# A graph network on one Trainium2 core: the second q projection and the second layer's neighbour sums as seven block products, a chunk transposed elsewhere, other banks for the root products

## The chip, the cores and the metric

The kernel runs on one core of one Trainium2 chip. A core has five engines with instruction streams of their own: TensorE (PE) multiplies matrices, VectorE (DVE) and ScalarE (ACT) do elementwise work and read PE's results out of its accumulation memory (PSUM, eight banks of 512 fp32 columns per partition), GpSimdE (POOL) does elementwise work in SBUF and issues indirect transfers, and SyncE (SP) issues transfers. PE's weight loads are listed apart as PEld. The metric is device time in microseconds: the median of three runs is 746.15 us (744.75 to 747.71). All data are fp32.

## The reference

With N = 384 nodes of 1024 features, the program computes `x = x + attention(relu(layernorm(x)))` and then `x = x + rgcn(relu(layernorm(x)))`.

The attention has two projections in a row for each of q, k and v, all 1024 by 1024:

```python
q = x @ wq.T + bq
q2 = (q @ wiq.T + biq)          # likewise k, k2 and v, v2
scores = einsum(q2, k2) * scale + mask    # 16 heads of 64; mask from 12672 typed edges
out = softmax(scores) @ v2, then @ wo.T + bo
```

The graph network projects to 768 features (`w_in`), runs two layers, and projects back (`w_out`) with a layer norm. A layer is, for six relations whose weights are combinations of four bases,

```python
W = einsum('rb,bio->rio', comp, basis)
x = relu(sum over edges of (x[src] @ W[type]) / count + x @ root + bias) + h_in
x = batchnorm(x)                # over the 384 nodes, per feature
```

## The kernel before, in words

Activations are kept transposed, features on the partitions: a 1024-feature tensor is 8 chunks of 128 features by 384 nodes, a 768-feature one 6 chunks. PE, POOL, SP and DVE run in exactly the order in which the program issues instructions; ACT is ordered by the scheduler in the first part of the program and by hand in the rest.

**Block products.** Many products are done as two by two blocks with seven instead of eight block multiplications (the Strassen-Winograd form): the inputs are halved over the contraction and over the 192 + 192 nodes, and two output chunks stand beside each other. The sums of weights (S, four, `output_sums`, line 367) and of activations (T1 to T4, `node_sum`, line 360) are made by DVE ahead of the products. Four of the seven products share accumulations in the banks pa, pb, pc, and the results are read out between them: ACT copies with the bias (lines 491, 492, 495, 512) and DVE additions (497, 503, 505). The last product of a part, with T4, is kept as `rest` and issued two products into the next part (line 493), after DVE's addition of line 503 has freed its bank. k, k2 and v are done so (loop at line 475; `multiply`, line 374, issues four matmuls of 192 columns). q and q2 are done by `project` (line 384), in whole products: per part of 256 output features, 2 x 8 matmuls of 384 columns (line 395).

**The adjacency.** The generator `edge_steps` (line 173) interleaves the building of two tables with the projections: each `fill(1)` runs one step. `find_cells` (line 232, DVE, two times 4 to 12 comparisons of 128 by 128 per call) finds the edges that hit the same cell; its results feed 198 indirect transfers on POOL (`put_mask`, line 261, and `put_count`, line 266). SP clears the tables (line 271) and loads the keys (line 238) in the same steps. The mask is read back for the softmax (lines 305 to 315); the counts become A, loaded by lines 657 to 661, divided per relation by `share` (line 335: PE sums, DVE reciprocal, POOL multiplication at line 342) and combined into At for the four bases by `mix` (line 319, on DVE, the first relation on ACT).

**Transition.** After attention, the output projection (line 616, the last half row in two pieces at line 688) adds to x row chunk by row chunk; each row chunk of 128 nodes is normalised into xn and transposed by PE with `relu_T` (line 157) into h2T, copied by ACT and DVE. The w_in products (`first_products`, line 718, and the loop from 731) need h2T.

**The layers** (loop at line 827). For each basis, H = x times basis, again in seven block products in five banks (lines 832 to 867), kept as 3 node chunks by 768 features. Then the root product into six banks pr, one for each output chunk (line 880; banks are taken from a ring, leaving out the bank `kept` of the pending `rest`), and on top, in the same banks, the neighbour sums: for each output chunk 12 matmuls of 384 columns over 4 bases and 3 node chunks (line 895, `add_neighbours`), first bases 0 and 1 for all chunks, then 2 and 3. As each chunk ends, ACT adds the bias and takes the Relu into `u` (line 905), DVE adds the input and normalises (lines 906 to 918). `go_between` puts the shares and mixes between the products. After the second layer come the output products (line 939), the layer norm and the store (line 954).

Weights pass through five buffers in the order of `wload`, issued by SP, which waits where a buffer is not free.

Of the kernel before, what the change touches and what calls it, by code (L numbers as in the profile page):

```python
# [51 lines left out]
def gnn_kernel(ctx: ExitStack, tc: tile.TileContext, out, x, edges, chunks, cols, rows, small,  # L52
# [294 lines left out]
    with ExitStack() as inner:  # L347
# [36 lines left out]
        def project(w, src, bias, name, on_part=None, on_start=None):  # L384

            dst = act_tile(name)
            for part in range(4):
# [12 lines left out]
                for o in range(2):  # L400
                    oc = part * 2 + o
                    nc.scalar.activation(dst[:, oc, :], ps[o][:, :N], AF.Identity,
                                         bias=cols_sb[:, bias + oc:bias + oc + 1])
                if on_part:
                    on_part(part)
                fill(1)
# [9 lines left out]
        with tc.tile_pool(name="edge", bufs=1, side="right") as ep:  # L416
# [32 lines left out]
            q = project(wq, hT, BQ, "q", on_start=last_chunk)  # L449
# [5 lines left out]
            plan = [(*i, part) for i in (("k", wk, BK), ("k2", wik, BIK), ("v", wv, BV)) for part in range(4)]  # L455
# [9 lines left out]
            def at_the_end(part):  # L465
                if part == 3:
                    for i in (1, 2, 3, 4):
                        node_sum(T, i, hT, sum_tile(i))
                    prepare()

            q2 = project(wiq, q, BIQ, "q2", at_the_end)
# [3 lines left out]
            for n, (name, w, bias, part) in enumerate(plan):  # L475
                src = made["k"] if name == "k2" else hT
# [4 lines left out]
                if n == 2:  # L481
                    nc.sync.dma_start(boB, rows[R_BO:R_BO + 1, :].to_broadcast([P, D]))
                if n < 10:
                    fill(1)
# [34 lines left out]
            k2, v = made["k2"], made["v"]  # L519
# [158 lines left out]
        for t in range(NT):  # L678
            last = t == NT - 1
            for half in range(2):  # L680
# [29 lines left out]
                add_y(half * 512, ps)  # L710
            norm(t, xn[:, t, :], *row_spread(st), parts=2 if last else 1)
            if not last:
                output_sums(a[t], S[t])
            if t:
                relu_T(h2T, t - 1, xn[:, t - 1, :])
# [49 lines left out]
    with tc.tile_pool(name="conv", bufs=1) as cp:  # L765
# [61 lines left out]
        for l in range(L):  # L827

            H_ = []
            rest = lambda: None  # L830
            for b in range(B):
                H_.append(cp.tile([P, NT, DC], F32, tag="H", name="H", bufs=4))
                hs = [[H_[b][:, n, i * HC:(i + 1) * HC] for i in range(2)] for n in range(NT)]
                pe, pf, pb, pc, pa = [next_bank("ps_g")[:, :N] for _ in range(5)]
                kept = ring[-1]
# [41 lines left out]
            pr = [next_bank("ps_c", [i for i in range(8) if i != kept])[:, :N] for _ in range(KC)]  # L877
            for k in range(KC):
                for o in range(KC):
                    nc.tensor.matmul(pr[o], w[k // 2][:, k % 2, o * P:(o + 1) * P], XT[:, k, :], start=(k == 0), stop=False)  # L880
                if k == 0:
                    rest()
                go_between(l, B, k)
            if l + 1 < L:
                w = load_basis(l + 1, 0)
            else:

                rowsB = late.tile([P, 3, D], F32, tag="A", name="rowsB")
# [3 lines left out]
            def add_neighbours(o, bs):  # L892
                for b in bs:
                    for n in range(NT):
                        nc.tensor.matmul(pr[o], H_[b][:, n, o * P:(o + 1) * P], At[:, b, n, :],  # L895
                                         start=False, stop=(b == B - 1 and n == NT - 1))

            for o in range(KC):
                add_neighbours(o, (0, 1))
            for o in range(KC):  # L900
                add_neighbours(o, (2, 3))
                ps = pr[o]
                c = l * KC + o
                u = cp.tile([P, N], F32, tag="u", name="u", bufs=2)
                nc.scalar.activation(u, ps, AF.Relu, bias=cols_sb[:, CB + c:CB + c + 1])  # L905
                nc.vector.tensor_tensor(XN[:, o, :], u, XT[:, o, :], ALU.add)  # L906
# [6 lines left out]
                nc.scalar.activation(sc[:, 0:1], sc[:, 0:1], AF.Sqrt)  # L913
                nc.vector.reciprocal(sc[:, 0:1], sc[:, 0:1])
# [4 lines left out]
                if o == 2 and l + 1 < L:  # L919
                    T = weight_sums(w)  # L920
# [7 lines left out]
        w = [wload(w_out[part], "w_out") for part in range(3)]  # L928
        for t in range(NT):
            hf = cp.tile([P, NT * DC], F32, tag="H", name="hf", bufs=4)[:, :D]  # L930
# [86 lines left out]
```

## Time and profile before

| | |
|---|---|
| median of three runs | 746.15 us |
| profiled execution, its own time | 747.49 us |
| its span | 745.7 us |
| mean granted PE clock | 0.994 |
| q projection on PE | about 13 to 56.9 us |
| q2 | 56.9 to 98.2 us |
| k, k2, v | 98.2 to 211 us |
| second v, attention | 211 to 312 us |
| output projection, transposes, w_in products | 312 to 388 us |
| layer 0: basis products, root, neighbours | 388 to 480, 477 to 506, 506 to 552 us |
| layer 1: the same | 552 to 641, 636 to 661, 661 to 707 us |
| output products, norm, store | 707 to 746 us |

How to read the profile: the first part of its page has the busy time of each engine; a digit in its second part is the busy share of a fortieth of the span in tenths. A row of the groups gives line, engine, operation, output and inputs, shapes and count, then the busy time, the mean of one in ns, and the engine's idle time ahead of them. A row in order of time gives start, duration (both us), engine, line, operation and count, and in brackets how long the engine was idle before it and what ended that. A row of windows gives, for a stretch, each engine's busy time with the count of instructions, then the granted PE clock, the DMA share and GB/s. A matmul of fp32 leaves two records. Ends of matmuls are modelled, so starts are the surer measure of pace.

### The profile page before, as it was taken

What the parts mean: (1) busy time and instruction counts of PE and PEld (TensorE: products, weight loads), DVE (VectorE), ACT (ScalarE), POOL (GpSimd) and SP (SyncE); (2) the same over time, 40 slices, a digit from 0 to 9 for tenths busy, and PEclk for the clock granted to TensorE, in tenths of its full rate; (3) what the DMA queues carried; (4) which work ended last, traced back from release to release, by engine and by line L of the source; (5) the groups of instructions that cost most, each with busy time, mean ns of one, the idle gap of its engine ahead of it and who ended that gap; (6) DMA issues with size and microseconds to landing.
All of it is one profiled execution on the core that took longest, in us unless ns stands there. A gap on an engine that the chain in (4) does not pass through costs nothing.

```text
span 745.7 us, 7797 instructions
## 1 busy us (share of the span) xinstructions
PE 724.6 (97%) x2820; PEld 471.6 (63%) x2820; DVE 435.3 (58%) x1161; ACT 141.8 (19%) x324; POOL 321.0 (43%) x242
## 2 busy tenths in 40 slices
PE   8999999999999999999899999899999999999995
PEld 7755589999964444446885555555555555555543
DVE  5878518878405499444524699980287766000655
ACT  3301021111102377410121130100022111000200
POOL 1355767778786787587774464210000000210000
PEclk9999999999999999999999999999999999999999
DMA  7797677644356322624428943321003312700001
GB/s 294 254 346 247 190 183 210 202 148 112 114 145 208 57 2 2 212 1 85 86 1 208 277 149 128 127 84 43 0 1 127 113 67 82 289 1 0 0 29 56
DMA packets 40532, 90.94 MB, mean 122 GB/s; under 512 B 19644, under 2 KB 27680, under 8 KB 36270
## 3 DMA queue, kind: packets, MB, share of 16 engines
q1 hardware_dynamic: 18478, 79.62, 30.4%
q0 software_dynamic: 21008, 8.42, 10.3%
q10 hardware_dynamic: 1008, 2.41, 0.8%
q8 instruction: 22, 0.36, 0.2%
q14 instruction: 16, 0.13, 0.0%
HBM read 79.27 MB, written 11.16 MB: 121 GB/s over the span
## 4 chain that ended last, share of the span: by engine, by line
PE 87%; DVE 10%; issue 1%; ACT 1%; DMA 0%; DVEq 0%; ACTq 0%
PE ps_c L895 12%; PE ps_g L846 12%; PE ps_q L395 11%; PE ps_g L840 9%; PE ps_k L377 7%; PE ps_c L880 6%; PE ps_v L525 6%; PE ps_y L616 5%; PE ps_f L939 4%; PE ps_v L377 4%; PE ps_s L564 3%; PE ps_x L377 3%; PE ps_o L609 2%; PE ps_pT L598 2%; DVE same L250 2%; DVE At L326 2%
## 5 line engine op out<-in xcount | busy, mean ns | idle before, releaser
L266 POOL DMA_INDIRECT atab<-count,at x99 | 159.2, 1608 | 55.8 <-DMA atab<-count,at 30.0
L261 POOL DMA_INDIRECT mtab<-m_val,at x99 | 102.3, 1034 | 58.5 <-issue 23.5
L895 PE MATMUL ps_c<-At,H 128*128 128x384 f32 x288 | 93.2, 486 | 0.0
L895 PEld LDWEIGHTS ps_c<-At,H 128*128 128x128 f32 x288 | 54.7, 190 | 38.2
L927 POOL TENSOR_TENSOR x_sb<-x_sb,rowsB 128x1024 f32<-128x1024 f32 x3 | 6.9, 2342 | 159.9 <-DMA rowsB<-in_rows 159.9
L326 DVE SCALAR_TENSOR_TENSOR At<-A,small_sb,At 128x1152 f32<-128x1152 f32 x40 | 62.9, 1635 | 0.0
L840 PE MATMUL ps_g<-T,S 128*128 128x384 f32 x144 | 49.1, 486 | 0.0
L846 PE MATMUL ps_g<-w_c,XT 128*128 128x384 f32 x144 | 48.0, 487 | 0.9 <-DVE H L861 0.9
L846 PE MATMUL ps_g<-w_c,XN 128*128 128x384 f32 x144 | 47.6, 486 | 0.0
L395 PE MATMUL ps_q<-hT,w_q 128*128 128x384 f32 (+1 forms) x160 | 43.4, 436 | 1.4 <-ACT hT L90 1.4
L525 PE MATMUL ps_v<-w_v,v 128*128 128x512 f32 x96 | 41.9, 594 | 0.0
L395 PE MATMUL ps_q<-q,w_q 128*128 128x384 f32 x128 | 41.4, 486 | 0.0
L846 PEld LDWEIGHTS ps_g<-w_c,XT 128*128 128x128 f32 x144 | 27.2, 190 | 20.1 <-DVE H L861 1.5
L846 PEld LDWEIGHTS ps_g<-w_c,XN 128*128 128x128 f32 x144 | 27.4, 190 | 19.1
L840 PEld LDWEIGHTS ps_g<-T,S 128*128 128x128 f32 x144 | 27.4, 190 | 19.1
L395 PEld LDWEIGHTS ps_q<-hT,w_q 128*128 128x128 f32 x160 | 30.2, 200 | 14.1 <-ACT hT L90 1.7
L906 DVE TENSOR_TENSOR XN<-u,XN 128x384 f32<-128x384 f32 x6 | 3.4, 558 | 56.3 <-ACT u L905 56.3
L395 PEld LDWEIGHTS ps_q<-q,w_q 128*128 128x128 f32 x128 | 24.3, 190 | 17.0
L616 PE MATMUL ps_y<-w_o,attT 128*128 128x512 f32 x80 | 35.0, 595 | 0.0
L377 PE MATMUL ps_k<-T,S 128*128 128x192 f32 x192 | 35.0, 326 | 0.0
L342 POOL TENSOR_TENSOR A<-A,rn 128x1152 f32<-128x1152 f32 x6 | 20.1, 3354 | 30.7 <-DVE rn L341 30.7
L577 DVE CUSTOM_DVE_ANT_0 s<-ps_s,mask 128x384 f32<-128x384 f32 x48 | 24.5, 548 | 14.3 <-PE ps_s L564 14.3
(212 smaller groups left out, 1184.2 us busy)
## 6 DMA issues: line engine op xcount, KB each, us to landing
w_c<-in_basis SPq DMA_DIRECT2D x24, 768.0 KB, 6.1
atab<-zero SPq DMA_DIRECT2D x12, 576.0 KB, 7.6
A<-atab POOLq DMA_DIRECT2D x10, 576.0 KB, 10.2
w_c<-in_root SPq DMA_DIRECT2D x6, 768.0 KB, 6.0
w_q<-in_wq SPq DMA_DIRECT2D x4, 1024.0 KB, 11.6
w_q<-in_wiq SPq DMA_DIRECT2D x4, 1024.0 KB, 12.6
w_k<-in_wk SPq DMA_DIRECT2D x4, 1024.0 KB, 5.7
w_k<-in_wik SPq DMA_DIRECT2D x4, 1024.0 KB, 6.2
```

The lines of the kernel that those rows point to most:

```text
L261: nc.gpsimd.indirect_dma_start(mtab[c // PER][:, :], bass.IndirectOffsetOnAxis(at[:, 0, c:c + 1], 0), m_val[:, c:c + 1], None)
L266: nc.gpsimd.indirect_dma_start(atab[0 if i < 18 - DEALT else i % 2][:, :], bass.IndirectOffsetOnAxis(at[:, 1, c:c + 1], 0), count[:, 1, c: ...
L326: nc.vector.scalar_tensor_tensor(At[:, b], A[:, r], w, At[:, b], ALU.mult, ALU.add)
L377: nc.tensor.matmul(ps, a[:, k, :], b[:, k, :], start=start and k == 0, stop=(k == 3), skip_group_check=not start)
L395: nc.tensor.matmul(ps[o][:, c], wt_[:, k, o * P:(o + 1) * P], src[:, k, c], start=(k == 0 and c.start == 0), stop=(k == KD - 1 and c.stop ...
L525: nc.tensor.matmul(ps, v[:, k, t * P:(t + 1) * P], w[k // 4][:, k % 4, :], start=(k == 0), stop=(k == KD - 1))
L616: nc.tensor.matmul(ps, attT[:, k, t * P:(t + 1) * P], w_o[half][k // 4][:, k % 4, :], start=(k == 0), stop=(k == KD - 1))
L840: nc.tensor.matmul(ps, x[:, c], y(c), start=start and c == 0, stop=(c == 2), skip_group_check=not start)
L846: nc.tensor.matmul(ps, block(XT, n, i)[:, c], w[c][:, i, o * HC:(o + 1) * HC], start=(first and c == 0), stop=(c == 2 and (i == 1 or ps is ...
L880: nc.tensor.matmul(pr[o], w[k // 2][:, k % 2, o * P:(o + 1) * P], XT[:, k, :], start=(k == 0), stop=False)
L895: nc.tensor.matmul(pr[o], H_[b][:, n, o * P:(o + 1) * P], At[:, b, n, :], start=False, stop=(b == B - 1 and n == NT - 1))
L939: nc.tensor.matmul(p, XT[:, k, t * P:(t + 1) * P], w[k // 2][:, k % 2, c0:c1], start=(k == 0), stop=(k == KC - 1))
```

## The change

1. `project` is used for q only. q2 becomes the first of the names in the block-product loop: 16 parts instead of 12, with weights prepared one part ahead. The T sums over q are made in `project`'s callback (T1 after part 2, the others and the first S after part 3, behind that part's `fill`), those over hT at the end of q2 as at the end of k2. The `fill` steps keep their place in the count: four in q, then one a part.
2. `relu_T` of the middle chunk of h2T is issued after the first half of the last row's output product, and so ahead of that row's last two pieces and its normalisation.
3. The four H tiles become one. The root products leave out two banks of the pending basis product instead of one.
4. In both layers ACT writes the biased sum into XN instead of `u`. In the second layer, the neighbour sums become seven block products for each pair of output chunks: contraction halved into bases 0, 1 and 2, 3; nodes into 192 + 192. Sums of At (T1 to T4) and of H (four a pair, made one pair ahead) are made by DVE; `take` adds a block product from its bank into XN; the Relu is a step of its own on ACT, and the batch norm of a chunk is split into `measure` and `normalise_layer`, placed between the takes. The freed tiles A, hT and mask8 hold the sums.

```diff
-                if on_part:
-                    on_part(part)
-                fill(1)
+                fill(1)
+                if on_part:
+                    on_part(part, dst)
...
-            q = project(wq, hT, BQ, "q", on_start=last_chunk)
...
-            plan = [(*i, part) for i in (("k", wk, BK), ("k2", wik, BIK), ("v", wv, BV)) for part in range(4)]
+            plan = [(*i, part) for i in (("q2", wiq, BIQ), ("k", wk, BK), ("k2", wik, BIK), ("v", wv, BV)) for part in range(4)]
...
-            def at_the_end(part):
+            def sums_of_q(part, q):
                 if part == 3:
-                    for i in (1, 2, 3, 4):
-                        node_sum(T, i, hT, sum_tile(i))
                     prepare()
-
-            q2 = project(wiq, q, BIQ, "q2", at_the_end)
+                for i in {2: (1,), 3: (2, 3, 4)}.get(part, ()):
+                    node_sum(T, i, q, sum_tile(i))
+
+            q = project(wq, hT, BQ, "q", sums_of_q, on_start=last_chunk)
...
-                src = made["k"] if name == "k2" else hT
+                src = {"q2": q, "k2": made.get("k")}.get(name, hT)
...
-                if n == 2:
+                if n == 6:
                     nc.sync.dma_start(boB, rows[R_BO:R_BO + 1, :].to_broadcast([P, D]))
-                if n < 10:
+                if n < 14:
                     fill(1)
...
                 add_y(half * 512, ps)
+                if last:
+                    relu_T(h2T, t - 1, xn[:, t - 1, :], (0, 1))
...
-            if t:
-                relu_T(h2T, t - 1, xn[:, t - 1, :])
+            if t == 1:
+                relu_T(h2T, 0, xn[:, 0, :], (0, 1))
...
-                kept = ring[-1]
+                kept = ring[-2:]
...
-            pr = [next_bank("ps_c", [i for i in range(8) if i != kept])[:, :N] for _ in range(KC)]
+            pr = [next_bank("ps_c", [i for i in range(8) if i not in kept])[:, :N] for _ in range(KC)]
...
+            def begin(o, func=AF.Identity):
+                c = l * KC + o
+                nc.scalar.activation(XN[:, o, :], pr[o], func, bias=cols_sb[:, CB + c:CB + c + 1])
+
+            if l + 1 < L:
+                for o in range(KC):
+                    add_neighbours(o, (0, 1))
+                for o in range(KC):
+                    add_neighbours(o, (2, 3))
+                    begin(o, AF.Relu)
+                    normalise_layer(*measure(o))
+                    if o == 2:
+                        T = weight_sums(w)
+            else:
...
+                nc.vector.tensor_tensor(T1, q(0, 1), q(0, 0), ALU.subtract)
+                nc.vector.tensor_tensor(T2, q(1, 1), T1, ALU.subtract)
+                T3 = q(0, 1)
+                nc.vector.tensor_tensor(T3, q(1, 1), q(0, 1), ALU.subtract)
+                nc.vector.tensor_tensor(T4, q(1, 0), T2, ALU.subtract)
...
+                pa = first_of(0)
+                for p in range(pairs):
+                    times(pr[2 * p][:, :HN], h(2 * p, 1), q(1, 0))
+                for o in range(KC):
+                    begin(o)
+                take(0, 0, pa)
+                ready = None
+                for p in range(pairs):
+                    last = p == pairs - 1
+                    sums = iter(()) if last else feature_sums(p + 1)
+                    o0, o1 = 2 * p, 2 * p + 1
+                    pc = next_bank("ps_c")[:, :HN]
+                    times(pc, S[p][0], T1, True)
+                    take(o1, 1, pc)
+                    if ready:
+                        normalise_layer(*ready)
+                    next(sums, None)
+                    times(pa, S[p][1], T2)
+                    take(o0, 1, pa)
+                    next(sums, None)
+                    times(pc, S[p][3], q(1, 1))
+                    take(o0, 1, pc)
+                    ready = measure(rectify(o0))
+                    if last:
...
+                    times(pa, S[p][2], T3)
+                    take(o1, 1, pa)
+                    normalise_layer(*ready)
+                    for _ in sums:
+                        pass
+                    following = first_of(p + 1)
+                    times(pa, h(o1, 1), T4)
+                    take(o1, 0, pa)
+                    take(o1 + 1, 0, following)
+                    ready = measure(rectify(o1))
+                    pa = following
```

## The prediction

> **What bounds the kernel now.** I read the busy shares first, then the costliest groups, then the order of time on TensorE (PE), then the queues that feed it. The first two lines are engine shares and PE by fortieths of the span.
>
> ```profile
> PE 724.6 (97%) x2820; PEld 471.6 (63%) x2820; DVE 435.3 (58%) x1161; ACT 141.8 (19%) x324; POOL 321.0 (43%) x242
> PE   8999999999999999999899999899999999999995
> ```
>
> PE is never idle for long: its waits by name come to 12 us of the 745.7 us span. So a part of the change is worth what it takes out of PE's stream, less the waits that it puts there. The two groups that the change rewrites:
>
> ```profile
> L895 PE MATMUL ps_c<-At,H 128*128 128x384 f32 x288 | 93.2, 486 | 0.0
> L395 PE MATMUL ps_q<-q,w_q 128*128 128x384 f32 x128 | 41.4, 486 | 0.0
> ```
>
> A source matmul leaves two records. 144 records of the second layer's L895 run from 660.80 for 46.44 us: 322.5 ns a record, 645 ns a matmul of 384 columns. The same arithmetic with 192 columns runs in the k projection; PE in order of time there (start, us, what):
>
> ```profile
> 98.22 1.46 PE L377 MATMUL ps_k<-hT,w_k 128*128 128x192 f32 x8
> 99.52 2.76 PE L377 MATMUL ps_k<-T,S 128*128 128x192 f32 x16
> ```
>
> Starts are 1.30 us apart per eight records: 162.5 ns a record, 325 ns a matmul. Seven half-width products for eight therefore cost 7/8 x 325/322.5 = 0.882.
>
> **A rule against it.** The Trainium skill, page "TensorE: Matmul & The Clock Gate", section "Back-to-back issue gap", says that in a stream of weight loads and matmuls both set the spacing, so narrow matmuls fall behind their own streaming time. A load here lasts 190 ns, more than 162.5. If it set the pace, 112 + 126 matmuls (476 records) would cost 27.5 ns more each, 13.1 us, and the gain below would be gone. But in the windows, from 98.4 to 116.0, loads and matmuls are both busy all the time at the 162.5 ns pace:
>
> ```profile
> 98.40:116.00 17.60, 17.60 (x110) 17.60 (x110) 4.88 (x11) 3.53 (x8) 12.28 (x11) 1.00 0.65 167
> ```
>
> The loads overlap one another; I use 162.5.
>
> **Part 1, q2 in block products.** Before: 64 matmuls x 645 ns = 41.3 us. After: 4 parts x 7 products x 4 = 112 x 325 ns = 36.4 us: **-4.9 us**. Added on VectorE (DVE), per part: four weight sums (0.68 us each, 0.61 apart: 2.5 us) and three additions (0.35); once, four sums over q (0.95 each); the four over hT move from the start to the end of q2. That is some 18 us more DVE work between 43 and 106 us. Where it lies:
> - Entry. DVE ends find_cells(3) at 51.7 now; with T1 of q (0.95) ahead of it, about 52.7. S of part 0 is done at 55.2 (its weights were issued at 37.2 and land in about 12.6). T2 needs q's last chunk, copied 57.14 to 57.72, so it is ready at 58.7, T3 at 59.6, T4 at 60.5. PE, free at 56.9, has two products of 1.30 before it needs T2, at 59.5. Nothing waits; with find_cells(3) late by more than 3 us, PE would.
> - find_cells(4) and find_cells(5) run at 56.9 and 79.6 now, in DVE time that is otherwise empty. In the new order they stand among q2's additions, which free PE's banks. The one in part 2 lies as find_cells(6) does in k today, where PE waited 0.31: **+0.3**.
> - The hand-over q2 to k is new. Its model is the hand-over k to k2, first DVE, then PE:
>
> ```profile
> 135.43 0.95 DVE L364 TENSOR_TENSOR T<-k 128x768 f32<-128x768 f32 x1
> ...
> 138.84 0.75 DVE L241 TENSOR_SCALAR cells<-keys 128x1152 int32<-128x1152 int32 x1
> ...
> 146.54 0.35 DVE L503 TENSOR_TENSOR k<-k,ps_k 128x192 f32<-128x192 f32 x1
> ```
>
> ```profile
> 146.95 1.57 PE L377 MATMUL ps_k<-T,w_k 128*128 128x192 f32 x8 [1.19 <-DVE k L503]
> ```
>
> Behind the T sums, S and a find_cells of 9 rows (138.84 to 145.41, 6.57 us), the L503 addition is late and PE's T4 product waits 1.19. At q2 to k the step holds find_cells(5), 12 rows; one of that size took 118.19 to 126.63, 8.44. 1.19 + 1.87 = **+3.1 us**. Behind it on PE stand only that part's other products, whose readers on ACT and DVE have time. Ends: 0 if DVE arrives 3 us earlier, 4 if its sums run late.
>
> Part 1: -4.9 + 0.3 + 3.1 = **-1.5**. The moved steps issue the same loads, clears and key loads on SP; each weight load only stands one fill earlier, and keys 4 move behind the last q2 load (46.8), to land near 60 for a use at 77. POOL's scatters wait for find_cells results: find_cells(4) will be done at 85 for a first scatter at 91.7, find_cells(5) at 105 for 116.
>
> **What an earlier PE meets.** POOL issues 198 scatters without pause and cannot follow PE:
>
> ```profile
> 388.99 1.55 POOL L266 DMA_INDIRECT atab<-count,at  x1 [0.30 <-issue]
> 396.99 1.36 POOL L659 DMA_DIRECT2D A<-atab  x1 [6.45 <-PE ps_g L846]
> ...
> 430.31 1.00 POOL L333 TENSOR_TENSOR sum<-sum,A 128x384 f32<-128x384 f32 x1
> ```
>
> The tightest meeting is share(2): its sum is ready at 431.3, PE uses it at 436.08. Slack 4.8 us, against the 1.5 + 2.8 = 4.3 that parts 1 and 2 bring by then: nothing is absorbed, narrowly. Earlier, mask8 is finished at 235.1 and first used at 239.37: slack 4.3 against part 1's 1.5.
>
> **Part 2, the middle chunk.** Now its transposes (354.91) and their copies, behind the last normalisation on DVE, precede the first product:
>
> ```profile
> 354.91 1.04 PE L162 MATMUL ps_h<-ident,xn 128*128 128x128 f32 x8
> 358.65 2.84 PE L377 MATMUL ps_x<-h2T,w_x 128*128 128x192 f32 x16 [2.71 <-issue]
> ```
>
> After: the transposes (0.87) stand at 348.0, their copies end near 350.4 under 6.9 us of L688 products. Those end at 355.8, the first products run to 358.4, and DVE's chain to the first half of xn (355.11 to 357.45 now, 0.87 later) ends at 358.3. The last transposes then end at 359.3; now 362.2. **-2.8 us** (2.4 if the second half is waited for in full).
>
> **Part 3, root banks.** In layer 0 the fourth root product waits 2.20 us for L853, which stands behind two At mixes on DVE. Followed through the ring of banks, the new set still puts that bank fourth and swaps only the fifth and sixth (free by 482.25, used at 482.2). **0**, +-0.1. Here the skill's clock rule bears too (same page, Part 1: half clock after about 3.4 us of idleness). The trace differs; in these windows the third number from the end is PE's granted clock:
>
> ```profile
> 478.00:481.00 3.00, 0.80 (x4) 0.19 (x2) 3.00 (x3) 0.00 (x0) 1.18 (x1) 0.96 0.71 291
> 481.00:482.00 1.00, 1.00 (x2) 0.70 (x3) 1.00 (x3) 0.00 (x0) 0.00 (x0) 0.50 0.00 0
> ```
>
> An idle time of 2.20 was followed by half clock to 484.2, some 1.8 us lost; 2.71 at 356 was not. By the rule the new 3.1 us wait costs nothing more, by this row 1.8. I take 0, by the row nearest in length, and keep 1.8.
>
> **Part 4, neighbours of layer 1.** 72 x 645 = 46.4 us become 3 pairs x 7 x 6 = 126 x 325 = 41.0: **-5.5**. The four sums of At (1152 elements, 1.3 each from the slope between 0.68 at 512 and 0.95 at 768) and the first pair's four (0.95) are 9 us, under the root products from 641 to 660.8, where DVE is empty. Inside, DVE has per pair six additions (0.35), four sums (0.95) and two of these chains (the batch norm of one chunk):
>
> ```profile
> 688.54 0.56 DVE L906 TENSOR_TENSOR XN<-u,XN 128x384 f32<-128x384 f32 x1 [52.30 <-ACT u L905]
> ...
> 691.15 0.48 DVE L918 TENSOR_SCALAR XN<-XN,sc 128x384 f32<-128x384 f32 x1
> ```
>
> 3.1 us each, plus about 0.6 waiting for the new Relu on ACT: 2.1 + 3.8 + 6.2 + 1.2, less overlap of issue, near 12.5 us against PE's 7 x 1.95 = 13.65. Laid out step by step, each addition is in time by 0.1 to 1 us; with every DVE duration 10% longer PE loses 1.4, with 20% longer 3.2. The output product starts with chunks 0 to 3 (6.9 us), and chunk 5 is normalised 4.8 after PE's last product (3.8 now): covered.
>
> **Sum.** -1.5 - 2.8 + 0 - 5.5 = -9.8 us. The profiled execution (747.49, span 745.7) would be 737.7 with span 735.9; on the median 746.15 I predict **736.4 us**.
>
> **Rivals.**
> - DVE paces the neighbours (against: the layout above fits; for: slack of 0.1): gives back 2 to 4, 739.4. Chance 0.16.
> - The scatters end later, through the added two-input DVE sums or shifted transfers, and the 4.3 of parts 1 and 2 are absorbed before layer 0: 740.7. For: slack 0.5; against: DVE is itself late there (PE waits 0.93 and 2.20 on it), which hides a late share. 0.12.
> - No hand-over wait, perhaps no half clock: 731.5 to 733.3. 0.08.
> - Weight loads pace the narrow products, in q2 and neighbours alike: -9.8 + 13.1, **749.5, slower**. It eats the whole gain from 183 ns a record; the k row speaks against. 0.03.
> - The middle chunk's gain reappears as a wait for xn: 739.2; DVE's chain would have to be 2.6 us longer. 0.03.
> - The forecast: 0.58.
>
> From about 0.5% (3.7 us) a measurement can tell a change. Only the loads case is slower, mostly by more than that; where two of the small losses meet, the time ends within, 0.04. Low: 733.0 (no hand-over wait). High: 741.0 (scatters absorb). Faster 0.94, same 0.04, slower 0.02.
>
> **What would show it.** PE's stream of 112 and 126 half-width matmuls at 162.5 ns a record; a wait on L503's successor of about 3 us at the second k part; no 2.7 us gap before the first w_in product; waits in the neighbours summing under 1 us; the 2.20 wait unchanged. Wrong if share(2) or L853 gains a wait as long as the early gain, if the neighbours' waits on the additions exceed 2 us, or if q2's entry waits.

## The result and the profile after

The changed kernel takes **736.71 us** (median of four runs, 735.77 to 738.39) against 746.04 (744.75 to 747.71) for the kernel before on the same chip: a ratio of 0.9874, 95% interval 0.9848 to 0.9900. The forecast was 736.4. The profiled execution has a span of 734.0 us; before it was 745.7. All medians and ratios here and below leave out the runs of a kernel that took over 1.5% longer than its fastest run.

The engine shares and PE by fortieths of the span, from the page of the changed kernel: PE is as full as before (97%), so the time left PE's stream. 11.1 us less of busy PE, 37.6 us more of busy DVE.

```profile
PE 713.5 (97%) x3024; PEld 496.8 (68%) x3024; DVE 472.9 (64%) x1228; ACT 147.2 (20%) x338; POOL 323.3 (44%) x242
...
PE   8999989999999999999999999899999999999995
```

**The neighbours of layer 1.** PE in order of time: the root products end, and 252 half-width records follow without an idle time until the output products at 695.36 (start, us, what; an idle time would stand in brackets). The last two rows are those of before: where the neighbours begin and where the output products follow.

```profile
654.40 7.96 PE L947 MATMUL ps_c<-At,H 128*128 128x192 f32 x48
...
671.96 2.11 PE L947 MATMUL ps_c<-T,H 128*128 128x192 f32 x12
673.90 4.06 PE L947 MATMUL ps_c<-room,room 128*128 128x192 f32 x24
...
695.36 4.88 PE L1054 MATMUL ps_f<-w_out,XN 128*128 128x512 f32 x11
```

```profile
660.64 19.84 PE L895 MATMUL ps_c<-At,H 128*128 128x384 f32 x61
...
707.08 13.47 PE L939 MATMUL ps_f<-w_out,XN 128*128 128x512 f32 x31
```

695.36 - 654.40 = 41.0 us, 162.5 ns a record; before, 707.08 - 660.64 = 46.4.

**The middle chunk.** PE again. The transposes stand ahead of the L687 products, and between these and the w_in products there is no gap; before, 2.71 us.

```profile
347.01 1.04 PE L162 MATMUL ps_h<-ident,xn 128*128 128x128 f32 x8
347.88 7.07 PE L687 MATMUL ps_y<-w_o,attT 128*128 128x256 f32 x32
354.79 2.76 PE L377 MATMUL ps_x<-h2T,w_x 128*128 128x192 f32 x16
357.43 1.11 PE L162 MATMUL ps_h<-ident,xn 128*128 128x128 f32 x8
```

**The hand-over from q2 to k.** DVE in order of time, then PE, then the windows of PE's clock (the third number from the end).

```profile
95.89 0.95 DVE L241 TENSOR_SCALAR cells<-keys 128x1536 int32<-128x1536 int32 x1
...
104.24 0.17 DVE L255 TENSOR_TENSOR at<-off,own 128x12 int32<-128x12 f32 x1
104.33 0.95 DVE L364 TENSOR_TENSOR T<-hT,T 128x768 f32<-128x768 f32 x1
105.19 0.35 DVE L496 TENSOR_TENSOR k<-k,ps_k 128x192 f32<-128x192 f32 x1
105.46 0.34 DVE L502 TENSOR_TENSOR k<-k,ps_k 128x192 f32<-128x192 f32 x1
```

```profile
105.86 2.61 PE L377 MATMUL ps_k<-T,w_k 128*128 128x192 f32 x8 [2.92 <-DVE k L502]
```

```profile
106.00:108.00 2.00, 2.00 (x8) 2.00 (x9) 1.97 (x5) 0.00 (x0) 1.70 (x2) 0.56 0.13 1
108.00:110.00 2.00, 2.00 (x9) 2.00 (x8) 0.60 (x1) 0.42 (x1) 1.39 (x3) 0.59 0.20 17
110.00:112.00 2.00, 2.00 (x14) 2.00 (x13) 0.19 (x1) 0.42 (x1) 1.70 (x2) 1.00 0.81 266
```

The wait is the one forecast (3.1), for the reason forecast: find_cells(5) holds DVE from 95.89 to 104.4, and the additions that free PE's bank stand behind it. What was not booked is the half clock after it. The trace's record of the granted clock gives it 3.41 us, so it costs half of that, 1.7.

**The root bank** still waits, but no half clock follows this time:

```profile
476.18 2.31 PE L880 MATMUL ps_c<-XT,w_c 128*128 128x384 f32 x6 [2.19 <-DVE H L853]
```

A balance by stages, from the starts of PE's first product in each, in us (q2's last product is issued inside the k stage):

| stage | before | after | difference |
|---|---|---|---|
| start to q2 | 56.9 | 55.4 | -1.5 |
| q2, k, k2, v | 153.8 | 154.4 | +0.6 |
| second v, attention, output | 147.9 | 145.0 | -2.9 |
| w_in products | 29.7 | 29.7 | 0 |
| layer 0 to its neighbours | 117.5 | 115.1 | -2.4 |
| neighbours 0, layer 1 to its neighbours | 154.8 | 154.8 | 0 |
| neighbours 1 | 46.4 | 41.0 | -5.5 |
| output products to the end | 38.6 | 38.6 | 0 |

The sum is -11.7. Two rows are not the change's doing. In the first, the execution before happened to run its first 16 q records at half clock (4.52 us for 2.84, at 13 us); in the fifth, it had the half clock after the root wait, and a wait of 0.9 on L861 which the other lacks. The other rows come to -7.8. Half clocks of 3.41 us come and go from one execution to the next (the last section shows what decides), so the worth of the parts has to be found one by one.

### The profile page after: what moved, and what is told of

Same layout as the page of the kernel before. It is cut to its first block, busy times and chain, and to the rows that moved or that the text cites. A ratio compares the mean times of both kernels' runs of the same rounds, so it can differ in the third digit from the quotient of the medians.

```text
span 734.0 us, 8299 instructions
## 1 busy us (share of the span) xinstructions
PE 713.5 (97%) x3024; PEld 496.8 (68%) x3024; DVE 472.9 (64%) x1228; ACT 147.2 (20%) x338; POOL 323.3 (44%) x242
## 4 chain that ended last, share of the span: by engine, by line
PE 86%; DVE 11%; ACT 1%; issue 1%; DMA 1%; DVEq 0%; ACTq 0%
PE ps_g L846 13%; PE ps_g L840 10%; PE ps_c L897 6%; PE ps_c L880 6%; PE ps_q L395 6%; PE ps_v L524 6%; PE ps_k L377 6%; PE ps_c L947 6%; PE ps_v L377 5%; PE ps_y L615 5%; PE ps_f L1054 4%; DVE same L250 3%; PE ps_q L377 3%; PE ps_x L377 3%; PE ps_o L608 2%; PE ps_s L563 2%
## 5 line engine op out<-in xcount | busy, mean ns | idle before, releaser
L261 POOL DMA_INDIRECT mtab<-m_val,at x99 | 104.1, 1052 | 57.0 <-issue 24.4
L1041 POOL TENSOR_TENSOR x_sb<-x_sb,room 128x1024 f32<-128x1024 f32 x3 | 7.0, 2347 | 158.1 <-DMA room<-in_rows 158.1
L897 PE MATMUL ps_c<-At,H 128*128 128x384 f32 x144 | 46.6, 486 | 0.0
L395 PE MATMUL ps_q<-hT,w_q 128*128 128x384 f32 (+1 forms) x160 | 41.8, 422 | 1.4 <-ACT hT L90 1.4
L840 PEld LDWEIGHTS ps_g<-T,S 128*128 128x128 f32 x144 | 27.4, 190 | 19.1
L897 PEld LDWEIGHTS ps_c<-At,H 128*128 128x128 f32 x144 | 27.4, 190 | 19.1
L846 PEld LDWEIGHTS ps_g<-w_c,XN 128*128 128x128 f32 x144 | 27.4, 190 | 19.1
L395 PEld LDWEIGHTS ps_q<-hT,w_q 128*128 128x128 f32 x160 | 28.5, 190 | 14.1 <-ACT hT L90 1.7
L524 PEld LDWEIGHTS ps_v<-w_v,v 128*128 128x128 f32 x96 | 18.0, 190 | 22.6 <-issue 22.6
L377 PEld LDWEIGHTS ps_k<-T,S 128*128 128x128 f32 x192 | 32.7, 194 | 0.0
L1054 PE MATMUL ps_f<-w_out,XN 128*128 128x512 f32 (+1 forms) x84 | 31.1, 531 | 0.0
```

The lines of the kernel that those rows point to most:

```text
L261: nc.gpsimd.indirect_dma_start(mtab[c // PER][:, :], bass.IndirectOffsetOnAxis(at[:, 0, c:c + 1], 0), m_val[:, c:c + 1], None)
L377: nc.tensor.matmul(ps, a[:, k, :], b[:, k, :], start=start and k == 0, stop=(k == 3), skip_group_check=not start)
L395: nc.tensor.matmul(ps[o][:, c], wt_[:, k, o * P:(o + 1) * P], src[:, k, c], start=(k == 0 and c.start == 0), stop=(k == KD - 1 and c.stop ...
L524: nc.tensor.matmul(ps, v[:, k, t * P:(t + 1) * P], w[k // 4][:, k % 4, :], start=(k == 0), stop=(k == KD - 1))
L840: nc.tensor.matmul(ps, x[:, c], y(c), start=start and c == 0, stop=(c == 2), skip_group_check=not start)
L846: nc.tensor.matmul(ps, block(XT, n, i)[:, c], w[c][:, i, o * HC:(o + 1) * HC], start=(first and c == 0), stop=(c == 2 and (i == 1 or ps is ...
```

## Experiments

The theory at the start: each part is worth what it takes from PE's stream, less the waits named. The main rival: POOL's 198 indirect transfers ("scatters") end too late for a PE that arrives earlier, and give the gain of the first two parts back in layer 0. The first four kernels (each part alone, and the old bank rule) ran on one chip, here chip A, the other eight on another, chip B, in two sets; each is compared with runs of the kernel before on its own chip. That kernel took 748.59 us (744.67 to 755.78) on A and 746.17 on B in both sets. On A the spread is wide: there the ratio of two medians can differ by 0.4% from the ratio given, but lies inside its interval.

### One part alone

**q2 alone.** The kernel before with the first item of the change only:

```diff
-            q = project(wq, hT, BQ, "q", on_start=last_chunk)
...
-            plan = [(*i, part) for i in (("k", wk, BK), ("k2", wik, BIK), ("v", wv, BV)) for part in range(4)]
+            plan = [(*i, part) for i in (("q2", wiq, BIQ), ("k", wk, BK), ("k2", wik, BIK), ("v", wv, BV)) for part in range(4)]
...
-            q2 = project(wiq, q, BIQ, "q2", at_the_end)
+            q = project(wq, hT, BQ, "q", sums_of_q, on_start=last_chunk)
```

> The kernel before with the q2 block products alone. My theory (each part worth what it takes out of PE's stream, less its own waits): -4.9 us of products, +0.3 (find_cells(4)), +2.9 of wait at the hand-over from q2 to k, so -1.7 us, and about 0 if the half clock that followed this wait in the changed kernel (1.7 us) follows it here too; k starts 4.6 us earlier on PE, counted from the end of q, and v ends 1.7 (or 0) earlier. Rival (scatters set the start of layer 0): the gain seen at the end of v is gone by the root product of layer 0, POOL's last scatter stays at 389, total 0.

Measured, on chip A: 753.17 us (749.52 to 758.25), ratio 1.0085 (1.0055 to 1.0116), slower than either side had it. On PE, k starts 4.7 us sooner after q2's first product (1.3 of this is q2's last product, which now runs inside k), and the hand-over wait is 2.92, as expected. But from q2 to the second v PE needs 158.7 us, against 154.5 in the second run below. Part of this is waiting for ACT's reads of its banks:

```profile
163.87 1.57 PE L377 MATMUL ps_k<-T,S 128*128 128x192 f32 x8 [1.05 <-ACT k L494]
...
171.26 1.57 PE L377 MATMUL ps_k<-T,S 128*128 128x192 f32 x8 [0.62 <-ACT k L490]
```

Single reads by ACT come up to 5.3 us later, counted from the start of k, than in the second run, and the trace names nothing that held ACT. The loss does not need q2's change: on chip A the same stage takes 159.2 us with the neighbours alone, where q2 is as before (153.8), and 160.0 with the old bank rule, where the changed kernel has 154.4; with the chunk alone it is 154.1. What causes it stays open. The kernel was run again on chip B.

> Only the q2 part of the change, on another chip than the first time, when ACT stood still for some 5 us in the k and v stages without a wait that the trace names. Theory: q2 4.7 shorter, a hand-over wait of 2.9 after it, and mostly a half clock of 1.7 behind that, so the total is 744 to 746.5, no difference or up to 2 us faster. Rival (q2 in block products does delay k and v, by its transfers or by ACT's reads of half-width banks): 750 to 753 again, with the same stalls of ACT.

Measured: **745.94** (744.76 to 747.53), ratio 0.9997 (0.9982 to 1.0013). No such loss. PE's waits in k and v, by name (engine, tile and line, released by; us in all, times, longest), and the windows behind the longest:

```profile
PE ps_k L377 <- DVE k L502: 4.3, 3, 2.9
...
PE ps_v L377 <- DVE v L502: 1.1, 1, 1.1
```

```profile
108.00:110.00 2.00, 2.00 (x11) 2.00 (x10) 1.97 (x4) 0.42 (x1) 1.54 (x2) 0.68 0.08 0
110.00:112.00 2.00, 2.00 (x8) 2.00 (x7) 0.22 (x1) 0.18 (x1) 1.54 (x2) 0.50 0.95 180
```

From q2 to the second v it needs 154.5 us against 153.8. Seven products for eight save 4.9; the new waits (0.3 and 2.9) and the half clock (1.7) take it all back. By itself this part is worth nothing on chip B.

**The middle chunk alone**, the kernel before with:

```diff
                 add_y(half * 512, ps)
+                if last:
+                    relu_T(h2T, t - 1, xn[:, t - 1, :], (0, 1))
...
-            if t:
-                relu_T(h2T, t - 1, xn[:, t - 1, :])
+            if t == 1:
+                relu_T(h2T, 0, xn[:, 0, :], (0, 1))
```

> The kernel before with the middle chunk's transposes moved alone. My theory: the 2.71 us gap before the first w_in product goes, total -2.8 us, carried through to the end. Rival 1 (the last normalisation is the real limit): a wait for xn of the same size before the last transposes, total 0. Rival 2 (scatters): the gain is lost between 388 and 480, total 0.

Measured: 746.12 us (742.56 to 750.75), ratio 0.9985 (0.9958 to 1.0012). The interval reaches from -3.1 us to +0.9, so the total alone does not exclude the theory's -2.8; the trace does. The gap was gone (output projection to w_in products 44.1 us against 47.0), and the 2.9 us came back in layer 0. PE's idle times there at the sums and on DVE's addition L863, then POOL at its last scatter:

```profile
418.28 0.91 PE L338 MATMUL ps_cnt<-sum,ones 128*128 128x384 f32 x2 [0.40 <-POOL sum L333]
433.92 0.91 PE L338 MATMUL ps_cnt<-sum,ones 128*128 128x384 f32 x2 [1.17 <-POOL sum L333]
455.04 5.83 PE L848 MATMUL ps_g<-w_c,XT 128*128 128x384 f32 x12 [4.08 <-DVE H L863]
```

```profile
391.58 1.63 POOL L266 DMA_INDIRECT atab<-count,at  x1 [0.30 <-issue]
399.18 1.36 POOL L659 DMA_DIRECT2D A<-atab  x1 [5.97 <-PE ps_g L842]
```

PE waits for the sums that POOL makes of the loaded counts, and then 4.08 us for DVE, whose mixes of At need the same counts. (Line numbers are those of each kernel: L863 here is the addition of L861 before, two lines having been added above it, and L855 is L853.) The waits at the sums are in neither trace of before and after; that on the addition was 0.93 before and is absent after. With the root wait, 0.62 here and 2.20 before, PE is idle for 6.3 us of layer 0 against 3.1: half of the loss lies at the sums, half with DVE. This is the rival's mechanism: layer 0 from its first product to the neighbours takes 121.3 us here, 117.5 before.

**The neighbours alone**, the kernel before with items 3 (one H tile, two banks left out) and 4:

```diff
-                kept = ring[-1]
+                kept = ring[-2:]
...
+            if l + 1 < L:
...
+            else:
...
+                    times(pc, S[p][0], T1, True)
+                    take(o1, 1, pc)
```

> The kernel before with the second layer's block products, the single H tile and the new root banks, without the q2 and chunk changes. My theory: the neighbour products of layer 1 take 41.0 instead of 46.4 us, total -5.5 us; no wait of PE on the additions over 0.3. Rival (DVE paces): 43 to 45 us, total -2 to -4. Rival (weight loads pace): 47.9 us, total +1.4.

Measured: 746.29 us (739.68 to 750.58), ratio **0.9934** (0.9890 to 0.9978), an interval from -1.6 to -8.2 us around the forecast's -5.5. The second layer's neighbours take 41.0 us instead of 46.4, with no wait on an addition (first and last rows of the stage on PE):

```profile
666.37 7.96 PE L946 MATMUL ps_c<-At,H 128*128 128x192 f32 x48
...
707.32 13.04 PE L1053 MATMUL ps_f<-w_out,XN 128*128 128x512 f32 x30
```

### The root banks

The changed kernel with the bank rule of before, and with layer 0's late bank moved to sixth place:

```diff
-                kept = ring[-2:]
+                kept = ring[-1:]
```

```diff
+            if l == 0:
+                pr.append(pr.pop(3))
```

> The changed kernel with one bank left out for the root products, as before. My theory: the fourth root product of layer 0 waits for the L853 addition in either set, 2.2 us, so the time is the changed kernel's within 0.3 us (ratio to before 0.987). Rival (the banks are worth the wait that they were changed for): the wait is longer here, 3 us or more, and the time 1 to 2.5 us above the changed kernel's.

> The changed kernel with the bank that waits for the L853 addition taken for the sixth root product of layer 0 instead of the fourth. My theory (the 2.2 us wait is that of this one bank): the wait shrinks by two products, 1.3 us, to 0.9, total -1.3. Rival (DVE sets the end of layer 0's mixes and PE only waits elsewhere): the 1.3 us come back before the neighbour sums, total 0.

Measured, the bank rule of before on chip A: 744.44 us (739.6 to 747.18), ratio 0.9943 (0.9916 to 0.9970). This is some 5 us above the expected 0.987. The changed kernel itself was not run on chip A, and this trace has a loss of 5.6 us between q2 and the second v, so the total decides nothing about the banks. Layer 0 does: root products to neighbours take 27.4 us in it and 27.7 in the changed kernel, with no half clock in either. Bank last, on chip B: 739.54 us (738.3 to 742.61), ratio 0.9918 (0.9895 to 0.9940), where the changed kernel itself ran at 738.26. The waits of layer 0's root products in the one and the other:

```profile
PE ps_c L880 <- DVE H L853: 2.0, 1, 2.0
```

```profile
PE ps_c L882 <- DVE rn L340: 2.9, 1, 2.9
```

The choice of banks is worth nothing in these traces: 2.0 us of wait with the old rule, 2.19 with the new. Nor can the wait be moved by taking its bank last: PE then waits at the bank of DVE's next reader, the reciprocal of L340. What is late is DVE, not a bank, and the gain of 1.3 that I had expected of moving it was wrong.

### How much room the additions have

The changed kernel with the statistics of each chunk of layer 1 taken three times, which adds 12 readings to DVE's stream:

```diff
+                for _ in range(2 * l):
+                    nc.vector.bn_stats(st, XN[:, o, :])
```

> The changed kernel with bn_stats of each chunk of the second layer done three times instead of once (+1.2 us of DVE work in each of six chains; the result is unchanged). My theory (DVE has some 1 us per pair to spare against PE's 13.65): the neighbour products of layer 1 take 45.4 us instead of 41.0 by the step by step layout, total +4.4, with waits of PE on the additions. If DVE has far more room than I worked out: under +1. If it were already the pace: +7.2, the added work of all six chains.

Measured: 742.6 us (740.3 to 746.69), ratio 0.9954 (0.9938 to 0.9971). The neighbours grew from 41.0 to 44.9, by 4.0 before rounding (the layout gave 4.4), and PE waits where it didn't before:

```profile
682.92 2.22 PE L949 MATMUL ps_c<-At,room 128*128 128x192 f32 x12 [0.81 <-DVE XN L981]
...
690.11 2.22 PE L949 MATMUL ps_c<-T,H 128*128 128x192 f32 x12 [0.62 <-DVE XN L981]
```

So the step-by-step layout is about right: DVE fits into PE's time with little to spare, and an addition to its stream shows at once.

### What an earlier PE meets

The hand-over waits come from DVE additions behind find_cells. If each `fill` of parts 4, 8 and 12 is issued after the additions, they should go; the changed kernel itself was run beside it.

```diff
-                if n < 14:
+                if n < 14 and n not in (4, 8, 12):
                     fill(1)
...
+                if n in (4, 8, 12):
+                    fill(1)
```

> The changed kernel itself, as the base for the other runs on this chip: 736.7 us, a ratio to before of 0.987; the same waits, 2.9 us at the hand-over from q2 to k and 2.2 at the fourth root product of layer 0. Whether half clock follows them may differ.

> The changed kernel with the three fill steps of the first parts of k, k2 and v (find_cells 5, 7 and 9 with them) issued after that part's additions instead of ahead of them. My theory of the hand-over (the additions stand behind find_cells): the waits of 2.92, 1.12 and 1.14 us become 0.3 each at most, and the half clock after the first goes: v ends 4 to 6 us earlier. POOL's slack at the third share is 5.9 us in the changed kernel, so the total falls by 4 to 5.5. Rival (scatters do not follow PE): the same at the end of v, but a new wait of PE before or at the shares of layer 0, total -1 to -2. Rival (find_cells late for POOL): POOL waits on DVE at its first scatter of find_cells(5), last scatter later, total up.

Measured: the changed kernel 738.26 us (736.79 to 740.87), ratio 0.9902 (0.9879 to 0.9924); with the late fills **740.40** (738.16 to 743.10), ratio 0.9927 (0.9903 to 0.9952). The second v projection starts 3.5 us sooner, at 206.3 (one wait of 2.3 is left, where two find_cells meet), and layer 0 takes it all back. PE in layer 0:

```profile
411.10 0.91 PE L338 MATMUL ps_cnt<-sum,ones 128*128 128x384 f32 x2 [0.86 <-POOL sum L333]
431.23 0.91 PE L338 MATMUL ps_cnt<-sum,ones 128*128 128x384 f32 x2 [1.15 <-POOL sum L333]
452.37 5.61 PE L848 MATMUL ps_g<-w_c,XT 128*128 128x384 f32 x12 [4.10 <-DVE H L863]
```

The three waits of the chunk-alone kernel again, the second and third within 0.02 us (here, too, L863 is the addition of L861). In layer 0 PE is idle for 6.8 us, where the changed kernel beside it has 2.5, all of it on DVE; of the 4.3 more, 2.0 lie at the sums and 2.3 with DVE. In the two kernels the last scatter is issued 7.4 and 8.3 us after layer 0's first product; in the changed kernel, in its two traces, 0.5 and 2.1. From these traces I formed a rule: layer 0's neighbours start at the later of two times, the first basis product plus about 115 us (PE's own order) or the last scatter plus about 112. (The 115 contain the 2 to 3 us that PE waits for DVE there in any case. A half clock on the way adds 1.7 to either.)

To test it, the last six count transfers are left out of the late-fill kernel and of the changed kernel, so that the graph layers miss six columns of edge counts:

```diff
-        for i in range(EC - PER + DEALT):
+        for i in range(EC - PER + DEALT - 6):
             put_count()
```

and a third kernel cuts each later find_cells in two: the half for the mask is issued where the whole was, and `second_half` issues the half for the counts after the additions of the part, so that no addition stands behind more than half of one:

```diff
-                find_cells(max(3, step // 2 + 1))()
+                halves.append(find_cells(max(3, step // 2 + 1)))
...
                     node_sum(T, 3, follow, sum_tile(3))
+                second_half()
```

> late_fill with the last six of the 99 count transfers left out: six columns of the edge counts are missing from the tables, so the attention is complete and the graph layers see fewer edges; PE's work is the same. Theory (layer 0 ends at the later of two things: PE's own order, about 115 us after its first basis product, or the last indirect transfer plus about 112): the last transfer is issued 6 x 1.85 = 11 us sooner, near 378, so that PE decides; its basis products start at 381, as in late_fill, the neighbours at 496 to 497 instead of 502.8, and the whole takes 733.5 to 736, 3.5 to 6 less than late_fill. The waits on POOL's sum (0.86, 1.15) and the 4.1 us wait on L863 are gone. Rival (DVE's order or the clock took the 3.5 us that late_fill won): the transfers are not what decides, the waits stay, 739 to 741.

> The changed kernel with the last six count transfers left out (six columns of the edge counts missing, PE's work the same). Theory: in the changed kernel PE decides already, narrowly, so the total is the same within 1 us, 737 to 738.3, and 0.5 to 1 lower only if its transfers end late in some executions. Rival (parts 1 and 2 are partly absorbed by the transfers in the changed kernel too, as the forecast's second rival had it): 2 to 4 us faster, 734 to 736.

> The changed kernel with each find_cells of the later steps cut in two: the half for the mask stays where it is, the half for the counts is issued after the additions of the same part. Theory (the hand-over waits are DVE additions standing behind a whole find_cells): each addition comes some 4 us sooner, the waits of 2.9, 1.1, 1.1 and 0.3 and the half clock go, and v2 starts 5 to 7 us sooner, at 203 to 205. Layer 0's basis products then start near 378 to 380, and the last transfer (384 to 389) plus 112 decides: neighbours at 496 to 501, total 732 to 737. Rival (the count half now delays the next part's additions by as much): v2 at 207 to 210, total 737 to 739.

Measured: late fills without six transfers **733.81** us (732.35 to 736.50), ratio 0.9849 (0.9830 to 0.9868); changed kernel without them 736.38 (735.41 to 737.10), ratio 0.9873 (0.9858 to 0.9889); split find_cells 737.87 (736.42 to 741.07), ratio 0.9910 (0.9891 to 0.9930).

In the late-fill kernel the answer is plain. The count transfers of that run (durations in ns, first and last start), and PE's only idle times between 380 and 500:

```profile
L266 POOL DMA_INDIRECT atab<-count,at x93: 1542/1552/1915, 79.6 to 375.6; - x93
```

```profile
379.85 1.57 PE L377 MATMUL ps_x<-T,w_x 128*128 128x192 f32 x8 [0.45 <-DVE XT L744]
472.43 3.90 PE L882 MATMUL ps_c<-XT,w_c 128*128 128x384 f32 x6 [2.00 <-DVE H L855]
```

PE's work is the same, the scatters end at 375.6 instead of 389.3, the waits on the sum and on L863 are gone, and the neighbours start at 497.4 instead of 502.8. Between the medians lie 6.6 us. (L855 is the root wait, as L853 is in the changed kernel.) The split kernel is the same test from the other side. All its hand-over waits are gone (no wait on these additions is left in its list), the second v starts at **201.1** instead of 209.8, layer 0 at 375.7 instead of 384.5, and the neighbours still start at 500.3. The idle times of PE (L870 is the addition of L861 there), and POOL at its last scatter:

```profile
408.26 0.91 PE L346 MATMUL ps_cnt<-sum,ones 128*128 128x384 f32 x2 [3.33 <-POOL sum L341]
428.60 0.91 PE L346 MATMUL ps_cnt<-sum,ones 128*128 128x384 f32 x2 [1.37 <-POOL sum L341]
449.74 5.83 PE L855 MATMUL ps_g<-w_c,XT 128*128 128x384 f32 x12 [4.09 <-DVE H L870]
```

```profile
387.86 1.55 POOL L272 DMA_INDIRECT atab<-count,at  x1 [0.30 <-issue]
395.59 1.36 POOL L667 DMA_DIRECT2D A<-atab  x1 [6.18 <-PE ps_g L849]
```

8.7 us of PE's time won before layer 0 are worth nothing in the end: in layer 0 PE is idle for 9.4 us, 4.7 of them at the sums, and 737.87 lies between the 736.71 and 738.26 of the changed kernel.

The rule against all of it (us; the neighbours' start with 1.7 taken off where a half clock lay between):

| kernel | first basis product | last scatter | +115 | +112 | measured |
|---|---|---|---|---|---|
| before | 388.4 | 389.0 | 503.4 | 501.0 | 504.1 |
| after | 384.5 | 385.1 | 499.5 | 497.1 | 499.6 |
| after, second run | 384.5 | 386.6 | 499.5 | 498.6 | 499.9 |
| q2 alone, second run | 388.9 | 386.9 | 503.9 | 498.9 | 503.4 |
| chunk alone | 384.2 | 391.6 | 499.2 | 503.6 | 503.7 |
| late fills | 381.1 | 389.3 | 496.1 | 501.3 | 501.1 |
| late fills, six left out | 381.2 | 375.6 | 496.2 | 487.6 | 495.7 |
| after, six left out | 386.2 | 376.8 | 501.2 | 488.8 | 500.8 |
| split find_cells | 375.7 | 387.9 | 490.7 | 499.9 | 498.6 |

The rows with six left out, with split find_cells and with q2 alone came after the rule. It holds to 1.3 us in these nine, and to 0.8 in the other five kernels of this study.

Leaving the six out of the changed kernel lies between the two expectations: 736.38, where 737 to 738.3 was the theory's and 734 to 736 the rival's. Its traced execution shows PE deciding; its median is 1.9 below that of the changed kernel on chip B and 0.3 below that of the result. In some executions, then, the transfers may cost the changed kernel a us or two; these runs do not settle how often.

## Why the prediction was right, and where not

The total was right to 0.3 us in the result and 1.9 in the second run of the changed kernel. By its own steps:

- **Neighbours, -5.5.** Right: 41.0 measured for 41.0, in the whole change and alone, and no wait. The layout's "slack of 0.1 to 1" for DVE is borne out by the run with more DVE work.
- **Weight loads as the slower rival.** It was given 0.03 and did not come: 162.5 ns a record held through all 126 matmuls of the neighbours, with loads of 190 ns in the same stretch.
- **Middle chunk, -2.8.** Right at its place (-2.9, in the whole change and alone). Whether it is kept is another matter, below.
- **Root banks, 0.** Right, and for the reason given: DVE is late, not the bank.
- **q2, -1.5.** This step failed, by some 2 us: it is worth +0.6 in the traces and 0 in the medians of its run alone on chip B. The products and the wait were right: 36.4 and 3.1 forecast; measured 36.7 (q2's stage of 35.7, less its wait of 0.3, and its last product of 1.3 in the k stage) and 2.9. The mis-sized term is the clock, 1.7 of the 2 us: "I take 0, by the row nearest in length, and keep 1.8." Seven of the eight traced executions with a hand-over wait of 2.9 to 3.0 show a half clock behind it. One row of a trace (the 2.71 that no half clock followed) was too little to choose by: of the four executions with that same 2.7 gap, one does have it.
- **"Nothing is absorbed, narrowly."** True of the changed kernel's two traces, but I took the slack at one meeting alone, share(2), 4.8 us. The other is DVE's mixes, made late by the same transfers, and there I counted DVE's lateness only as something that hides a late share. It does not hide it: DVE's two waits (0.93 and 2.20 before, 1.92 and 0.60 in the second run of the changed kernel) become 4.1 and 0.6 or 0.7 whenever the transfers are late, on top of 1.6 to 4.7 at the sums. By the rule above the neighbours are late once the last scatter stands more than 3 us behind the first basis product. Before the change it stood 0.6 behind: room for an estimated 2.4, not 4.8. No trace stands between 2.1 behind, where nothing is lost, and 7.4.
- **"POOL issues 198 scatters without pause."** Half right. Of the idle time before the 99 count transfers in the changed kernel, about 26 us is waiting for the landing of earlier transfers into the same table, and it varies, so the last scatter falls anywhere from 384 to 392. In the nine traced executions with q2 in block products and all transfers it came at 386.5 on average; in the three without, at 390.1. By the rule, this is how the whole change kept the chunk's 2.8 us which the chunk alone lost. What in q2's new form draws the transfers forward was not tried, and three executions are few. The totals of the parts alone (0, about 1 and about 5 us against 7.3 to 9.4 for the whole) fit this, but with intervals of 2 to 7 us they do not show it.

So the total is better than its steps, by luck. Part by part the traces give +0.6 - 2.9 - 5.5 = -7.8 us, 2 short of the forecast's -9.8, and -7.9 is what chip B has between its medians. The result has -9.3 between medians and -11.7 between the traced executions, and of the latter -1.5 at the start and most of -2.4 in layer 0 are half clocks and a wait that came with the execution, not with the change. On chip B, where the clock fell at the hand-over and once more at L861, the span was 736.0, within 0.1 of the forecast's 735.9, by the same luck.

## What to carry to other kernels

Before counting a gain, find the chain of another engine that ends beside it, here the scatters on POOL, and measure its slack at every meeting, not at the first: half of the loss came one engine further on, at DVE. A test for such a bound is cheap: shorten that chain, even by leaving work out, and see whether the lost gain comes back (6.6 us here). A DVE addition that frees a bank should not stand behind a long block of side work; cutting find_cells in two removed every wait of that kind, 8.7 us of PE's time. By the rule above this will pay once the transfers end earlier; the two were not run together. And a line number means something in one kernel only: the wait on L863 in one trace and that on L861 in another are for the same addition.

## What was unexpected of the hardware

The half clock comes in pieces of one length: each in the traces' record (but for the last, at the end of the program) lasts 3.41 us and costs 1.7. It follows waits of very different length, and not always: after the root wait of 2.0 to 2.2 us in five of eight traces, after 2.9 nearly always, after the waits of 1.9 and 4.1 us on the addition of L861 in all five traces that have them, and at the start of the q projection in 6 of 14. What decides can be read from the record. In each of the 14 traces the half clocks begin at whole multiples of 3.413 us from each other, on a grid that lies differently against the program each time. Cut by this grid from 8 us on, every stretch of a trace in which PE was busy for under 1.4 of the 3.41 us was followed by half clock, and none with over 1.6; between these, some. So a wait costs 1.7 us if enough of it falls into one stretch of the grid. The same gap of 2.7 us before the w_in products, in two stretches of the kernel before and two of the neighbours alone (PE's busy time is the second number):

```profile
354.47:357.88 3.41, 1.47 (x11) 1.13 (x9) 2.36 (x8) 0.69 (x2) 1.78 (x2) 1.00 0.92 290
357.88:361.30 3.42, 2.65 (x16) 2.68 (x17) 0.67 (x2) 0.00 (x0) 1.55 (x1) 1.00 0.64 166
```

```profile
361.39:364.81 3.42, 0.81 (x5) 0.84 (x6) 2.17 (x6) 0.69 (x2) 0.70 (x1) 1.00 1.03 306
364.81:368.22 3.41, 3.41 (x13) 3.41 (x12) 0.00 (x0) 0.00 (x0) 2.79 (x2) 0.50 0.29 45
```

Before, the grid cuts the gap in two and the clock stays (1.47 lies between the limits); alone, it lies inside one stretch and half clock follows. The one hand-over wait of 3.0 us without half clock is cut in the same way (PE busy for 1.83 us in the emptier stretch). The limits were read off afterwards, and PE's ends are modelled. The Trainium skill ("TensorE: Matmul & The Clock Gate", Part 1) puts the fall after an idle window of some 3.4 us; in these traces the length agrees, but a stretch with up to 1.5 us of work in it was enough.

Three of the four kernels traced on chip A lost 4 to 5.6 us between q2 and the second v for no reason that a trace names, and the fourth did not. The q2 part, judged by its run there, would have been called a loss of 0.85%; on chip B it was 0.03% the other way.
